# Two PSUM banks as one tile or as two: the weighted sums and the 3x3's products of an attention and convolution kernel

## The chip, the cores and the metric

The kernel runs on one core of a Trainium2 chip. The metric is the device time of one execution in microseconds (us). The runs before the change took 1933.58, 1933.69 and 1933.92 us; their median, 1933.69, is the time before.

## What is computed

The input x holds 8 images of 64 channels and 64 x 64 pixels in float32. Two layers follow each other:

```
# layer 0: attention over the 4096 pixels of each image
q, k, v = wq x + bq, wk x + bk, wv x + bv            # 64 x 64 weights
q, k    = q - mean(q), k - mean(k)                   # means over the pixels
out     = softmax(q^T k / 8) v                       # 4096 x 4096 scores
out    += (softmax(mean(q)^T k) v)                   # one row, added to every pixel
x       = x + out

# layer 1: binary convolutions with kernels of 1, 3 and 5
s = sum over k in (1, 3, 5) of bn_k(conv_k(sign(x + move_k), scale_k * sign(w_k - mean(w_k))))
gate = sigmoid(grouped linear map of mean(s) over the pixels)
x = s * gate + x
```

## The kernel before, in words

**Tiling.** Two images lie on the 128 partitions together, 64 channels each, so there are four pairs of images. A pair's 4096 queries are cut into eight blocks of 512 (`QB`), which makes 32 blocks, g = 0 to 31, in one long chain. Within a block the keys are taken 128 at a time in 32 steps (`NK`, index j).

**A step.** `scores` (lines 470 to 486) makes four matmuls of 64x64 weights and 512 columns into a PSUM tile of two banks; float32 matmuls appear twice in the records, so that a group of four in the code is a group of eight there. ScalarE takes the exponent of both banks in one instruction (line 485). `weighted` (lines 488 to 499) multiplies it with the values, in four matmuls of the same size, and adds the products over the 32 steps in the tile `acc`: two banks, one for each half h of the keys. VectorE adds up the exponents themselves (`summed`, line 508). Everything is written one step ahead: the scores of step j stand before the weighted sums of step j - 1, so the weighted sums of step 31 of a block come after the first scores of the next block.

**The hand-over between blocks.** `plan` (line 974) tells for each block what else stands at which step; the order of every engine's work is thus fixed by the program. At step 0 of block g these come, after the last weighted sums of block g - 1:

- `weighted_out` (lines 510 to 515): ScalarE copies the two banks of `acc` to SBUF, in one instruction of 128 x 1024 (line 515). The two halves are added together by VectorE some twelve steps later (`added`, line 582).
- `send` and `gather`: SyncE's DMAs for the sums of the exponents.
- `mix_rows` (lines 881 to 942): TensorE makes the queries of block g + 1 (line 460) and, from block 3 on, the convolution of block g - 3, as row products (line 703) of 256 columns in two interleaved sequences. One sequence has eight products S of the 5x5, the 1x1 (line 785), the twelve products of the 3x3 in the order A, B, S, D, three of each, and two more of the 5x5; the other has the 5x5's A, B and D. Each is made once for each image.
- The 3x3's A and B lie in the first bank of a tile, S and D in the second. This tile has the tag `acc`, of which the pool `ps_a` has one buffer: it is the same PSUM space as the weighted sums', which is empty between two blocks.
- When the 1x1 is done, `begin_rows` (line 729) has ScalarE scale it and put it in SBUF. When the last D product is recorded, `hold_rows` (lines 731 to 738) has ScalarE scale the whole 3x3 tile and put it in SBUF (line 734, 128 x 1024). VectorE adds the 5x5's products from PSUM (lines 744 and 750).

Then the scores of step 1 follow (line 474), and then the first weighted sums of block g (line 493), which write the tile with the tag `acc` again. Blocks 4, 12 and 20 have a small product ahead of these scores, for the means of the next pair (line 290), and blocks 8, 16 and 24 two, for the one-row softmax (line 363).

Dependencies are kept for each tile: an instruction that writes a tile anew waits for the last reader of the tile's former content, whichever of its banks that read.

**The end.** The last block is finished with the 2-D `mix` (line 830). Its attention result is copied out in two column parts (320 and 192 columns). For the first two blocks of output of the last pair, TensorE adds s * gate and x in a tile `pre` of two banks, also with the tag `acc` (lines 1103 to 1132): two products with the identity early on, two with the gate's diagonal at the very end, each followed by a copy by ScalarE (line 1131) and a store that ScalarE issues (line 1132). The other six blocks are done by VectorE (line 827) and stored by SyncE (line 828). A second path (lines 1171 to 1230) repeats the work with a safe softmax; it is skipped unless a sum went out of range.

Of the kernel before, what the change touches and what calls it, by code (L numbers as in the profile page):

```python
# [18 lines left out]
F32 = mybir.dt.float32  # L19
# [7 lines left out]
P = 128  # L27
C = 64
HH = 64
N = HH * HH  # L30
KS = (1, 3, 5)
QB = 512
# [12 lines left out]
def conv_seq_kernel(ctx, tc, x, wq, wk, wv, vecs, w1, w3, w5, wtap, gw, out):  # L45
    nc = tc.nc
# [3 lines left out]
    img = [slice(0, C), slice(C, P)]  # L50
# [6 lines left out]
    sm = ctx.enter_context(tc.tile_pool(name="small", bufs=2))  # L57
    dp = ctx.enter_context(tc.tile_pool(name="dram", bufs=2, space=bass.MemoryType.DRAM))
    ps_s = ctx.enter_context(tc.tile_pool(name="ps_s", bufs=2, space=PSUM))
    ps_a = ctx.enter_context(tc.tile_pool(name="ps_a", bufs=1, space=PSUM))  # L60
    ps_m = ctx.enter_context(tc.tile_pool(name="ps_m", bufs=2, space=PSUM))

    def m_tile(name):
        return ps_m.tile([P, QB], F32, tag="m", name=name)

    def load_x(name, rows, queues=(nc.sync,)):
        xt = xp.tile([P, N], F32, tag="x", name=f"x_{name}")
        for c in range(4):
            cols = bass.ts(c, N // 4)
            queues[c % len(queues)].dma_start(out=xt[:, cols], in_=xf[rows, cols])  # L70
        return xt
# [36 lines left out]
    ident = cp.tile([P, P], F32, tag="ident", name="ident")  # L108
# [42 lines left out]
    def warm(n):  # L151

        t = ps_s.tile([P, 2, QB], F32, tag="s", name="warm")[:, 0, :]
        for _ in range(n):
            nc.tensor.matmul(t[:, 0:P], ones, ones, start=True, stop=True)  # L155
# [89 lines left out]
    def n_products(k, name):  # L245
        return k if k == 3 or name == "D" else 2 * k
# [10 lines left out]
    class Pair:  # L257
# [229 lines left out]

        def weighted(self, qb, j, e):
            if j == 0:
                self.acc[qb] = ps_a.tile([P, 2, QB], F32, tag="acc", name=f"acc_{self.name}_{qb}")  # L490
            for b in range(2):
                for h in range(2):
                    nc.tensor.matmul(  # L493
                        self.acc[qb][img[b], h, :],
                        self.v[img[h], j, img[b]],
                        e[img[h], b, :],
                        start=(j == 0),
                        stop=(j == NK - 1),
                    )
# [10 lines left out]
        def weighted_out(self, qb, parts=(slice(0, QB),)):  # L510

            acc = self.acc[qb]
            self.acc[qb] = self.tile(fp, "o", qb, (P, 2, QB))
            for c in parts:
                nc.scalar.copy(self.acc[qb][:, :, c], acc[:, :, c])  # L515

# [209 lines left out]
            self.s[qb] = self.sum_tile(qb)  # L728
            nc.scalar.activation(self.s[qb], z, AF.Identity, bias=shift, scale=scale[:, 0:1])

        def hold_rows(self, qb, two):

            z = self.tile(sm, "es", f"z3_{qb}", (P, 2, QB))
            nc.scalar.activation(z, two, AF.Identity, scale=frac[3][:, 0:1])  # L734
            self.z3 = [
                z[:, i // 2, bass.ts(i % 2, QB // 2)].rearrange("p (j w) -> p j w", w=HH)
                for i in range(4)
            ]

        def add_rows(self, qb, a, b, s):  # L740
# [140 lines left out]
    def mix_rows(q, c):  # L881


        seqs = [[], []]
        if q is not None:
            for h in range(2):
                seqs[h].append((("q",), 0, 2.0))
        if c is not None:
            p, (r0, _, y) = c
            qb = r0 // ROWS  # L890

            def products(k, name):
                return [((k, name), i, 0.5) for i in range(n_products(k, name))]

            S = products(5, "S")
            three = [t for name in "ABSD" for t in products(3, name)]
            seqs[0] += S[:8] + [((1,), 0, 1.0)] + three + S[8:]
            seqs[1] += products(5, "A") + products(5, "B") + products(5, "D")
        order = []
        for h, seq in enumerate(seqs):  # L900
            at = 0.0
            for t in seq:
                order += [(at, h, b, t) for b in (h, 1 - h)]
                at += t[2]
        order.sort(key=lambda o: o[0:2])
        if q is not None:
            q[0].query_tiles(q[1])
        z, left = {}, {}
        for o in order:
            left[o[3][0]] = left.get(o[3][0], 0) + 1  # L910
        half = [slice(0, QB // 2), slice(QB // 2, QB)]
        for _, h, b, (n, i, _) in order:
            if n == ("q",):
                q[0].split_queries(q[1], b, h)
            else:
                if n not in z:
                    name = f"{p.name}_{qb}_{n[0]}"
                    if n == (1,):
                        z[n] = m_tile(f"z{name}")
                    elif n == (5, "D"):  # L920
                        z[n] = m_tile(f"z{name}d")[:, half[0]]
                    elif n[0] == 3:
                        z3 = ps_a.tile([P, 2, QB], F32, tag="acc", name=f"z{name}")
                        for j, m in enumerate("ABSD"):
                            z[3, m] = z3[:, j // 2, half[j % 2]]
                    else:
                        t = score_banks(f"z{name}")
                        z[5, "S"], z[5, "A"], z[5, "B"] = t[0][:, half[0]], t[1][:, half[0]], t[1][:, half[1]]
                if n == (1,):
                    p.conv_tap((r0, ROWS, y), [[z[n]]], b, 0, 0, 0, True, True)  # L930
                else:
                    p.row_product(z[n], b, *n, i, r0)
            left[n] -= 1
            if left[n] == 0 and n == ("q",):
                q[0].split_queries_out(q[1])
            elif left[n] == 0 and n == (1,):
                p.begin_rows(qb, z[n])
            elif left[n] == 0 and n == (3, "D"):
                p.hold_rows(qb, z3)
        if c is not None:  # L940
            p.add_rows(qb, z[5, "A"], z[5, "B"], z[5, "S"])
            p.z5d = z[5, "D"]
# [4 lines left out]
    def banks(pool, tag):  # L947
        def two(name):
            t = pool.tile([P, 2, QB], F32, tag=tag, name=name)
            return [t[:, 0, :], t[:, 1, :]]  # L950

        return two

    quarters = [slice(c * N // 4, (c + 1) * N // 4) for c in range(4)]
    acc_banks, score_banks = banks(ps_a, "acc"), banks(ps_s, "s")

    def misc_banks(name):
        return [m_tile(f"{name}_{h}") for h in range(2)]
# [5 lines left out]
    def attend(pairs):  # L964
# [9 lines left out]
        def plan(g):  # L974
# [17 lines left out]
            def both():  # L992
                q = block(g + 1) if g + 1 < n_blocks else None
                if g == 0:
                    mix(q, None)
                else:
                    mix_rows(q, rows(g - 3) if g >= 3 else None)
# [83 lines left out]
        for g in range(n_blocks):  # L1081
            pr, qb = divmod(g, NQ)
            at = plan(g)
            p = pairs[pr]
# [13 lines left out]
        p, b = pairs[-1], NQ - 1  # L1098
# [1 line left out]
        p.weighted_out(b, [slice(r0 * HH, r1 * HH) for r0, r1 in parts])  # L1100
        p.sums_wide(b)

        pre = ps_a.tile([P, 2, QB], F32, tag="acc", name="pre")
        for i in range(2):
            nc.tensor.matmul(pre[:, i, :], ident, p.x2[i], start=True, stop=False)
        warm(10)
        halves = [slice(r0 * HH, r1 * HH) for r0, r1 in parts]
        p.added(b, halves[0])
# [17 lines left out]
        diag_g = sm.tile([P, P], F32, tag="diag_g", bufs=1, name="diag_g")  # L1126
        nc.vector.tensor_scalar(diag_g, ident, p.gt, None, ALU.mult)
        rows_p = rows_of(n_pairs - 1)
        for i in range(2):
            nc.tensor.matmul(pre[:, i, :], diag_g, p.s[i], start=False, stop=True)  # L1130
            nc.scalar.copy(p.s[i], pre[:, i, :])
            nc.scalar.dma_start(out=of[rows_p, bass.ts(i, QB)], in_=p.s[i])
        for i in range(2, NQ):
            p.store(i, rows_p)
# [1 line left out]
    with tc.manual_schedule():  # L1136
        first = Pair("0", xt)
        warm(6)
        projection()
        warm(4)  # L1140
        first.mean_part(0, quarters[0])
        vectors()
        first.mean_part(1, quarters[1], True)
        first.mean_part(2, quarters[2])
        for c in range(2):
            first.mean_part(3 + c, slice(N * (6 + c) // 8, N * (7 + c) // 8), c == 1)
        first.query_tiles(0, score_banks)
        for b in range(2):
            first.queries(0, b)
        load_weights()  # L1150
        warm(18)
        first.mean_sum(5)
        first.mean_scores()
        first.mean_scores_out()
        first.queries_out(0)
        key_bias()
        first.value_weights()
        attend([first] + [None] * (n_pairs - 1))
# [12 lines left out]
    with tc.If(n_good < P):  # L1171
        neg = fp.tile([P, QB], F32, tag="e5", name="neg")
        nc.vector.memset(neg, 0.0)
        with tc.For_i(0, n_pairs * P, P) as row:
            rows = bass.ds(row, P)
            p = Pair("g", load_x("g", rows))
# [9 lines left out]
            for qb in range(NQ):  # L1186
                mix((p, qb), None)
                for h in range(QB // P):
                    part = sm.tile([P, 2, NQ], F32, tag="part", name=f"part_{qb}_{h}")
                    for kb_ in range(NQ):  # L1190
                        ps = ps_s.tile([P, 2, QB], F32, tag="s", name=f"px_{qb}_{h}_{kb_}")
                        for b in range(2):
# [4 lines left out]
                                start=True,  # L1197
                                stop=True,
# [90 lines left out]
```

## Time and profile before

The profile is of one execution on the chip. A busy share is the part of the span in which an engine had an instruction running; TensorE's matmuls overlap each other, and their ends are modelled.

| | before |
|---|---|
| median of 3 runs | 1933.69 us |
| the profiled execution's own time | 1934.02 us |
| its span, first to last instruction | 1931.8 us |
| TensorE busy | 1914.2 us, 20848 matmuls |
| VectorE busy | 1594.1 us |
| ScalarE busy | 1274.0 us, 1523 instructions |
| scores, line 474 | 8192 matmul records, 590 ns each |
| weighted sums, line 493 | 8192 matmul records, 590 ns each |
| exponents, line 485 | 1024 instructions, 1025 ns each |
| copies of the weighted sums, line 515 | 33 instructions, 31 of them 128 x 1024 at 1006 ns |
| copies of the 3x3's products, line 734 | 29 instructions, 1114 ns each |
| granted TensorE clock | 0.998 of full |

### The profile page before, as it was taken

How to read it: one execution, taken by the hardware profiler on the slowest of the kernel's cores; microseconds unless marked ns; L12 is line 12 of the kernel's file. 1: busy time of each engine (PE TensorE's matmuls, PEld its weight loads, DVE VectorE, ACT ScalarE, POOL GpSimd, SP SyncE). 2: the span in 40 equal slices, each digit the busy share in tenths (PEclk: the TensorE clock that was granted, in tenths of full speed). 3: DMA queues.
4: the chain of work that ended last, by engine and by line, in shares of the span. 5: the costliest groups of instructions: out<-in, count | busy, mean ns of one | idle time of the engine just before them, and what ended most of it. 6: DMA issues, size and time to landing. Idle time of an engine off the chain costs nothing.

```text
span 1931.8 us, 48355 instructions
## 1 busy us (share of the span) xinstructions
PE 1914.2 (99%) x20848; PEld 754.9 (39%) x20848; DVE 1594.1 (83%) x2066; ACT 1274.0 (66%) x1523; POOL 5.9 (0%) x26
## 2 busy tenths in 40 slices
PE   9999999999999999999999999999999999999997
PEld 4333343343333333343433333433443333333334
DVE  6878888889887888888888888898887888877876
ACT  5667766666666766666666676666666666666663
POOL 0000000000000000000000000000000000000000
PEclk9999999999999999999999999999999999999999
DMA  3021110110112110101101211011011011111111
GB/s 101 31 70 29 28 40 32 40 35 16 40 35 80 56 51 27 41 32 40 35 16 40 84 53 57 28 29 40 32 40 35 16 56 50 49 39 37 25 35 46
DMA packets 58998, 80.58 MB, mean 42 GB/s; under 512 B 15628, under 2 KB 40600, under 8 KB 58648
## 3 DMA queue, kind: packets, MB, share of 16 engines
q1 hardware_dynamic: 58024, 76.22, 12.9%
q8 instruction: 165, 2.70, 0.6%
q10 hardware_dynamic: 720, 1.18, 0.2%
q14 instruction: 57, 0.47, 0.1%
q0 software_dynamic: 32, 0.01, 0.0%
HBM read 39.27 MB, written 24.77 MB: 33 GB/s over the span
## 4 chain that ended last, share of the span: by engine, by line
PE 97%; DVE 1%; ACT 1%; DMA 0%; issue 0%; SPq 0%; DVEq 0%
PE ps L474 46%; PE acc L493 45%; PE z L703 4%; PE pv L313 1%; PE pq L460 1%; PE z L785 1%; ACT e L485 0%; DMA x<-in_x 0%; DVE es L508 0%; PE warm L155 0%; DVE r L576 0%; PE z_5d L703 0%; DMA out<-sb 0%; ACT o L515 0%; ACT rc_ck L418 0%
## 5 line engine op out<-in xcount | busy, mean ns | idle before, releaser
L485 ACT ACTIVATE e<-ps 128x1024 f32<-128x1024 f32 x1024 | 1049.7, 1025 | 597.8 <-PE ps L474 576.8
L508 DVE TENSOR_TENSOR es<-es,e 128x1024 f32<-128x1024 f32 x960 | 1171.2, 1220 | 187.6 <-ACT e L485 158.2
L474 PE MATMUL ps<-q,x 64*64 64x512 f32 x8192 | 1069.5, 590 | 0.9 <-DVE kb L165 0.9
L493 PE MATMUL acc<-e,v 64*64 64x512 f32 x8192 | 1065.2, 590 | 0.6 <-ACT e L485 0.3
L493 PEld LDWEIGHTS acc<-e,v 64*64 64x64 f32 x8192 | 307.6, 131 | 577.8 <-ACT e L485 305.9
L474 PEld LDWEIGHTS ps<-q,x 64*64 64x64 f32 x8192 | 312.2, 133 | 528.9 <-issue 278.0
L703 PE MATMUL z<-e,wt 64*64 64x256 bf16 x754 | 69.3, 270 | 0.1
L703 PE MATMUL z<-ec,wt 64*64 64x256 bf16 x754 | 69.4, 270 | 0.0
L744 DVE SCALAR_TENSOR_TENSOR sb<-z,scale,sb 128x256 f32<-128x256 f32 x29 | 14.0, 483 | 65.4 <-PE z L703 62.2
L703 PEld LDWEIGHTS <-wt 64*64 64x64 bf16 x1508 | 65.0, 105 | 0.4 <-issue 0.4
L703 PE MATMUL z<-ec,wc 64*64 64x256 bf16 x464 | 60.5, 270 | 0.0
L506 DVE TENSOR_TENSOR es<-e,e 128x1024 f32<-128x1024 f32 x32 | 39.2, 1225 | 24.5 <-ACT e L485 24.5
L703 PEld LDWEIGHTS <-wc 64*64 64x64 bf16 x1218 | 55.6, 106 | 4.8 <-issue 0.6
L619 ACT ACTIVATE s<-x,vec 128x512 bf16<-128x512 f32 (+2 forms) x66 | 46.1, 702 | 5.2 <-DVE x L587 5.2
L757 DVE TENSOR_TENSOR sb<-sb,es_z 128x256 f32<-128x256 f32 x116 | 43.9, 420 | 1.0
L703 PE MATMUL z<-e,wc 64*64 64x256 bf16 x319 | 44.4, 270 | 0.0
L734 ACT ACTIVATE es_z<-z,frac 128x1024 f32<-128x1024 f32 x29 | 32.3, 1114 | 16.3 <-PE z L703 16.3
L515 ACT COPY o<-acc 128x1024 f32<-128x1024 f32 (+2 forms) x33 | 32.3, 981 | 1.2 <-PE acc L493 1.2
L467 DVE TENSOR_SCALAR q<-pq,mx 128x256 f32<-128x256 f32 x30 | 14.5, 484 | 20.8 <-PE pq L460 20.8
L313 PEld LDWEIGHTS pv<-wx,x 64*64 64x64 f32 x1024 | 21.6, 134 | 17.8 <-issue 9.2
L703 PE MATMUL z<-s,wc 64*64 64x256 bf16 x145 | 25.4, 270 | 0.0
L587 DVE SCALAR_TENSOR_TENSOR x<-x,ou,x 128x512 f32<-128x512 f32 (+2 forms) x33 | 24.3, 735 | 1.2
(156 smaller groups left out, 743.6 us busy)
## 6 DMA issues: line engine op xcount, KB each, us to landing
es<-es SPq DMA_DIRECT2D x31, 512.0 KB
e_parts<-es SPq DMA_DIRECT2D x124, 128.0 KB
r<-rc SPq DMA_DIRECT2D x62, 128.0 KB
x<-in_x SPq DMA_DIRECT2D x15, 512.0 KB
out<-sb SPq DMA_DIRECT2D x28, 256.0 KB
ec<-e SPq DMA_DIRECT2D x29, 153.0 KB
xc<-in_x SPq DMA_DIRECT2D x60, 64.0 KB
ec<-e SPq DMA_DIRECT2D x29, 132.0 KB
```

Of the source, the lines that this page charges most:

```text
L313: nc.tensor.matmul(pv[img[h], b, i * w : (i + 1) * w], self.x[img[b], bass.ds((4 * g + i) * P + h * H, H)], self.wx[img[b], :], start=True ...
L474: nc.tensor.matmul(ps[img[h], b, :], self.x[img[b], bass.ds(j * P + h * H, H)], self.q[qb][img[b], :], start=True, stop=neg is None,)
L485: nc.scalar.activation(e, ps, AF.Exp, scale=1.0 / 8.0)
L493: nc.tensor.matmul(self.acc[qb][img[b], h, :], self.v[img[h], j, img[b]], e[img[h], b, :], start=(j == 0), stop=(j == NK - 1),)
L506: nc.vector.tensor_tensor(self.es[qb], self.first, e, ALU.add)
L508: nc.vector.tensor_tensor(self.es[qb], self.es[qb], e, ALU.add)
L515: nc.scalar.copy(self.acc[qb][:, :, c], acc[:, :, c])
L587: nc.vector.scalar_tensor_tensor(x2, x2, self.ou, self.x[:, bass.ts(qb, QB)][:, cols], ALU.add, ALU.add)
L619: nc.scalar.activation(sy[n][0][:, rows, pad : pad + HH], self.x2[qb][:, r0 * HH : r1 * HH].rearrange("p (h w) -> p h w", w=HH), AF.Sign, ...
L703: nc.tensor.matmul(z[img[b], :].rearrange("p (h w) -> p h w", w=HH), taps[img[h], c * C : c * C + C], src[:, first : first + 3 * step + 1 ...
L734: nc.scalar.activation(z, two, AF.Identity, scale=frac[3][:, 0:1])
L757: nc.vector.tensor_tensor(out, out, self.z3[i], ALU.subtract if (i, t) == (3, 1) else ALU.add)
```

## The change

The tile of two banks becomes two tiles of one bank each, with the tags `acc0` and `acc1`, wherever the tag `acc` was used: for the weighted sums, for the 3x3's products, and for `pre` at the end. The copy out of the weighted sums becomes two instructions of 512 columns, one for each bank. The 3x3's products are scaled and copied in two instructions too: the bank of A and B as soon as the last B product is recorded, the bank of S and D after the last D. Their place in SBUF stays one tile. The number and order of the matmuls stay.

```diff
         def weighted(self, qb, j, e):
             if j == 0:
-                self.acc[qb] = ps_a.tile([P, 2, QB], F32, tag="acc", name=f"acc_{self.name}_{qb}")
+                self.acc[qb] = acc_banks(f"acc_{self.name}_{qb}")
             for b in range(2):
                 for h in range(2):
                     nc.tensor.matmul(
-                        self.acc[qb][img[b], h, :],
+                        self.acc[qb][h][img[b], :],
...
             for c in parts:
-                nc.scalar.copy(self.acc[qb][:, :, c], acc[:, :, c])
+                for h in range(2):
+                    nc.scalar.copy(self.acc[qb][:, h, c], acc[h][:, c])
...
-        def hold_rows(self, qb, two):
-
-            z = self.tile(sm, "es", f"z3_{qb}", (P, 2, QB))
+        def hold_rows(self, qb, two, i):
+
+            if i == 0:
+                self.zh, self.z3 = self.tile(sm, "es", f"z3_{qb}", (P, 2, QB)), []
+            z = self.zh[:, i, :]
             nc.scalar.activation(z, two, AF.Identity, scale=frac[3][:, 0:1])
-            self.z3 = [
-                z[:, i // 2, bass.ts(i % 2, QB // 2)].rearrange("p (j w) -> p j w", w=HH)
-                for i in range(4)
+            self.z3 += [
+                z[:, bass.ts(t, QB // 2)].rearrange("p (j w) -> p j w", w=HH) for t in range(2)
             ]
...
-                        z3 = ps_a.tile([P, 2, QB], F32, tag="acc", name=f"z{name}")
+                        z3 = acc_banks(f"z{name}")
                         for j, m in enumerate("ABSD"):
-                            z[3, m] = z3[:, j // 2, half[j % 2]]
+                            z[3, m] = z3[j // 2][:, half[j % 2]]
...
-            elif left[n] == 0 and n == (3, "D"):
-                p.hold_rows(qb, z3)
+            elif left[n] == 0 and n in ((3, "B"), (3, "D")):
+                i = "BD".index(n[1])
+                p.hold_rows(qb, z3[i], i)
...
-    acc_banks, score_banks = banks(ps_a, "acc"), banks(ps_s, "s")
+    score_banks = banks(ps_s, "s")
+
+    def acc_banks(name):
+        return [ps_a.tile([P, QB], F32, tag=f"acc{h}", name=f"{name}_{h}") for h in range(2)]
...
-        pre = ps_a.tile([P, 2, QB], F32, tag="acc", name="pre")
+        pre = acc_banks("pre")
         for i in range(2):
-            nc.tensor.matmul(pre[:, i, :], ident, p.x2[i], start=True, stop=False)
+            nc.tensor.matmul(pre[i], ident, p.x2[i], start=True, stop=False)
...
-            nc.tensor.matmul(pre[:, i, :], diag_g, p.s[i], start=False, stop=True)
-            nc.scalar.copy(p.s[i], pre[:, i, :])
+            nc.tensor.matmul(pre[i], diag_g, p.s[i], start=False, stop=True)
+            nc.scalar.copy(p.s[i], pre[i])
```

## The prediction

> **What bounds the kernel now.** I read the page first, then the table of waits, then the timeline around the places where a block of 512 queries hands over to the next, then the same around the end. The page:
>
> ```profile
> PE 1914.2 (99%) x20848; PEld 754.9 (39%) x20848; DVE 1594.1 (83%) x2066; ACT 1274.0 (66%) x1523; POOL 5.9 (0%) x26
> ```
>
> TensorE is busy all the time, so what counts is time in which it could have started a matmul and did not. Busy time does not show that: each matmul record lasts longer than its distance from the next. The waits name the candidates (who waited for whom: us in total, times, longest):
>
> ```profile
> PEld acc L493 <- ACT e L485: 305.9, 955, 1.2
> ...
> PEld acc L493 <- ACT es_z L734: 22.2, 29, 0.9
> ```
>
> The second row is the wait that the change is about: the first weighted sum of a block waits for ScalarE to empty the 3x3's products (one allocation, both banks). But 22.2 us is idle time of the weight load, which is normally early; the first row has 305.9 us of it without harm. The timeline of one hand-over gives the true loss. Its columns are start, length, engine and line; first ScalarE's rows, then TensorE's:
>
> ```profile
> 779.64 1.01 ACT L515 COPY o<-acc 128x1024 f32<-128x1024 f32 x1
> 780.53 0.49 ACT L468 ACTIVATE q<-pq,nmx 128x256 f32<-128x256 f32 x1
> 781.07 0.78 ACT L729 ACTIVATE sb<-z,shift,scale 128x512 f32<-128x512 f32 x1
> 782.41 1.11 ACT L734 ACTIVATE es_z<-z,frac 128x1024 f32<-128x1024 f32 x1 [0.56 <-PE z L703]
> ```
>
> ```profile
> 782.55 1.03 PE L474 MATMUL ps<-q,x 64*64 64x512 f32 x6
> 783.58 1.09 PE L493 MATMUL acc<-e,v 64*64 64x512 f32 x8
> 784.49 1.04 PE L474 MATMUL ps<-q,x 64*64 64x512 f32 x8
> 785.34 1.04 PE L493 MATMUL acc<-e,v 64*64 64x512 f32 x8
> ```
>
> Undisturbed, groups of eight start 0.86 us apart (784.49 to 785.34), and a group starts 0.19 before the records of the one ahead end (784.49 + 1.04 = 785.53 against 785.34). The scores end at 782.55 + 1.03 = 783.58, so the weighted sums could start at 783.39. They start at 783.58, 0.06 after the copy ends at 783.52: 0.19 lost. The group after it follows 0.91 later, not 0.86: 0.05 more, seen whenever all eight loads go at once. Together **0.24 us per hand-over**.
>
> Where a small product stands between, nothing is lost: scores at 723.32, weighted sums 0.90 later, the next 0.86 after.
>
> ```profile
> 723.32 1.09 PE L474 MATMUL ps<-q,x 64*64 64x512 f32 x8
> 724.22 1.04 PE L493 MATMUL acc<-e,v 64*64 64x512 f32 x8
> 725.08 1.04 PE L474 MATMUL ps<-q,x 64*64 64x512 f32 x8
> ```
>
> Of the 29 blocks with 3x3 products (g = 3 to 31), six are like this (g = 4, 12, 20 with the means' scores, g = 8, 16, 24 with the unary sums). In the other 23 the timeline has the 0.91 after the weighted sums, each time.
>
> **What the Trainium skill says.** "Trainium Kernel Development and Optimization", Performance Expectations: matmul busy time is a bad measure, as matmuls are pipelined. The trace agrees: 99% busy with 0.24 us lost at 23 places. "ScalarE: Activation LUTs", What ACT_TABLE_LOAD costs: 186 ns + 0.833 ns a column, about 93 ns more for each pointer operand, and neighbours overlap by about 93 ns. The trace has 1114 ns for line 734 (1024 columns, one pointer; by the page 1132) and an overlap of 0.12 (copy at 779.64 for 1.01, next start 780.53). "PSUM — Partial Sum Buffer", PSUM bank collisions: two engines must not be in one bank and quadrant at once, different banks may be used together. That permits the split; no run here has shown it yet. "TensorE: Matmul & The Clock Gate", What's actually happening: after an idle window the clock is halved; the end of this trace agrees (part 4).
>
> **The change, part by part.** The order of instructions in the built program is the same on TensorE, VectorE and SyncE. ScalarE gets 62 more in the part that runs (33 copies of the sums, 29 of the products). TensorE gets one new ScalarE wait at the second weighted sum of a block and one at the first S product; the second of the last products (line 1130) loses its wait.
>
> 1. *The products' copy in halves.* The last D product starts at 782.09; A and B (bank 0) are complete six products of 0.11 earlier, at about 782.09 - 0.66 + 0.27 = 781.70. ScalarE is then in line 729 until 781.85 and idle until 782.41. So the first half starts at about 781.75, and nothing but the second half and the next exponent (783.64, set by the scores' end) is queued behind it. Half of line 734 is not in the trace: 0.59 (the plain 128x512 copy of line 321) to 0.78 (line 729, with two pointers). I take 1.114 - 512 x 0.833/1000 = 0.69. The first half ends at 782.44; the second starts when D is done, 782.41, and ends at 783.10. With 0.06 for the signal, bank 1 is free at 783.16, and at 783.25 with 0.78: both ahead of 783.39. The wait is gone, at either bound. Gain 0.24 in 22 blocks: 22 x 0.24 = 5.28 us.
>
> What is late next: the scores after these would start at 784.25 and need the score banks of the 5x5, whose last reader, VectorE's line 750, starts at 783.56 and takes 0.48, so 784.04, 0.10 for the signal at most: 0.11 to spare. Line 750 needs the second half too, now at 783.16. VectorE, 83% busy, catches up in each block (its sums wait 158.2 us for the exponents).
>
> 2. *The last block (g = 31)* has no queries ahead of the products, and there they wait for the sums' copy as well (ScalarE, then TensorE):
>
> ```profile
> 1839.71 1.01 ACT L515 COPY o<-acc 128x1024 f32<-128x1024 f32 x1
> ```
>
> ```profile
> 1840.42 0.61 PE L703 MATMUL z<-e,wt 64*64 64x256 bf16 x2
> 1840.77 0.29 PE L703 MATMUL z<-ec,wt 64*64 64x256 bf16 x1
> ```
>
> The pace of 0.11 breaks between 1840.42 and 1840.77, 0.05 after the copy ends. The products take 2.92 us to the next scores, 2.66 elsewhere. With bank 0 free at 1839.71 + 0.59 = 1840.30, A does not wait, and S (some 0.7 later) finds bank 1 free at 1840.79. Gain 0.26 + 0.24 = 0.50.
>
> 3. *The sums' copy in halves* elsewhere: 0.59 twice with 0.11 overlap, 1.07 for 1.01. The query half (line 468) starts 0.07 later. Its bank is next needed at 782.00, the queries a block later, and line 729 waits for the 1x1 (781.04). Nothing, covered by ScalarE's idle 0.69 a step; without that cover 31 x 0.07 = 2.2 us. At the very end, two copies of 320 columns (0.43 each) free the first addition at 1905.46 for 1905.39, and VectorE's chain stands on the path: -0.07.
>
> 4. *The last two products, in two tiles* (TensorE, SyncE's and ScalarE's stores, then the share of the 16 DMA engines in 40 slices of 1920 to 1931):
>
> ```profile
> 1920.48 1.12 PE L1130 MATMUL pre<-sb,diag_g 128*128 128x512 f32 x2 [0.83 <-DVE diag_g L1127]
> 1922.29 2.08 PE L1130 MATMUL pre<-sb,diag_g 128*128 128x512 f32 x2 [0.68 <-ACT sb L1131]
> ```
>
> ```profile
> 1923.77 1.25 SPq L828 DMA_DIRECT2D out<-es_j  x2
> ```
>
> ```profile
> 1925.01 0.35 ACTq L1132 DMA_DIRECT2D out<-sb  x1
> ```
>
> ```profile
> DMA  0000001798999999999999999963211300010100
> ```
>
> The second pair waits for the first copy and then takes 2.08 for 1.12, the halved clock that the skill tells of. Without the wait it starts at about 1921.4 and the last store is issued some 1.7 us sooner. But SyncE issues its own last until 1925.02, where ScalarE's ends at 1925.36, and the DMA engines are full from 1922 to 1927. So the gain is at most 0.34, at least nothing (no loss: the same bytes, none of them later). I take 0.2.
>
> Sum: 5.28 + 0.50 - 0.07 + 0.20 = **5.9 us**. The profiled execution took 1934.0 (span 1931.8 and 2.2 around it), 0.3 above the median of 1933.69: a span of 1925.9, a median of **1927.8** (-0.31%).
>
> **Rivals.** *Another wait takes over* (chance 0.15). VectorE's release of the 5x5's banks has only 0.11 to spare. If line 750 or its signal slips by 0.26, so 0.15 of the 0.24 is lost: 22 x 0.09 + 0.6 = 2.6 us, 1931.1. Against it: in this profile it already ends at 784.04 without help.
>
> *Nothing comes of it* (0.06). The 0.24 is given back inside each block, by VectorE not emptying the exponents' five buffers in time (that wait is 6.2 us in all now), or the two tiles still wait as one. Only the end's 0.1 remains: 1933.6. Against it: VectorE's slack, and the second weighted sum's own wait in the built program.
>
> *Slower* (0.06). ScalarE's fixed costs: if the first half is not released before D (the signal of B seen late), both halves run one after the other from 782.41: 0.58 + 0.69 = 1.27, ending 783.68 where the single one ended 783.52. That is 0.16 x 23 = 3.7 us, with the 0.07 of the end 1937.5. It decides from a first start later than 783.52 - 1.27 = 782.25. Against it: line 729 starts 0.03 after the 1x1's records end, so such signals are prompt.
>
> **How the numbers follow.** The forecast has 0.73: 0.67 within 1926.6 to 1930 (hand-over gain 0.17 to 0.29, the end 0 to 0.3), the rest at its lower edge. About 0.2% (3.9 us, so below 1929.8) is what a measurement of this kernel tells from no change. Faster by that: 0.72 of the forecast and 0.04 of the first rival, 0.76; within: 0.01, 0.11, 0.06 and 0.00, 0.18; slower: 0.06. The range goes to 1931.5 to take in the first rival.
>
> **What would show it.** Right: weighted sums 0.19 earlier after the scores and the 0.91 gone from behind them in 22 blocks; a first half at about 781.75 on the time base above; no row of weighted sums waiting for line 737 that costs a start; line 1130's second pair right behind the first. Wrong: first halves starting with D, or scores waiting for VectorE's line 753.

## The result and the profile after

The changed kernel takes 1928.79 us (median of 12 runs, 1927.98 to 1929.67), the kernel before 1933.66 us in the same series (median of 12, 1933.36 to 1934.51). The ratio is 0.9974, 95% interval 0.9966 to 0.9982: 0.26% faster, 4.9 us. The forecast was 1927.8.

The profiled execution took 1928.49 us, its span is 1926.3, 5.5 less than before. From its page, the busy times of the engines, then the two groups of copies (line, engine, operation, tiles, count; busy share or time, mean ns of one):

```profile
PE 1908.6 (99%) x20848; PEld 954.7 (50%) x20848; DVE 1592.5 (83%) x2066; ACT 1277.6 (66%) x1585; POOL 5.9 (0%) x26
...
L737 ACT ACTIVATE es_z<-z,frac 128x512 f32<-128x512 f32 x58 | 39.1, 687 | 0.0
L516 ACT COPY o<-acc 128x512 f32<-128x512 f32 (+2 forms) x66 | 34.4, 580 | 1.2 <-PE acc L493 1.2
```

The 62 more ScalarE instructions are there (1585 for 1523), and half of the products' copy takes 687 ns, where the forecast took 0.69. ScalarE is busy 3.6 us more, at no price. The table of waits of the changed kernel:

```profile
PEld acc L493 <- ACT e L485: 301.6, 955, 1.2
...
PEld acc L493 <- ACT es_z L737: 3.9, 22, 0.3
```

The second row was 22.2 us in 29 waits; what is left, 22 waits of 0.18 each, is a weight load that is early anyway. The hand-over that the prediction showed, now in the changed kernel, ScalarE and then TensorE (start, length, engine, line; `x2` is two instructions back to back):

```profile
778.39 1.07 ACT L516 COPY o<-acc 128x512 f32<-128x512 f32 x2
779.33 0.50 ACT L468 ACTIVATE q<-pq,nmx 128x256 f32<-128x256 f32 x1
779.82 0.78 ACT L730 ACTIVATE sb<-z,shift,scale 128x512 f32<-128x512 f32 x1
780.50 1.35 ACT L737 ACTIVATE es_z<-z,frac 128x512 f32<-128x512 f32 x2
```

```profile
781.17 0.60 PE L474 MATMUL ps<-q,x 64*64 64x512 f32 x2
...
781.30 1.03 PE L474 MATMUL ps<-q,x 64*64 64x512 f32 x6
782.03 1.15 PE L493 MATMUL acc<-e,v 64*64 64x512 f32 x8
782.89 1.15 PE L474 MATMUL ps<-q,x 64*64 64x512 f32 x8
783.75 1.15 PE L493 MATMUL acc<-e,v 64*64 64x512 f32 x8
```

The first half now starts behind line 730, 0.67 ahead of the scores, and both halves have ended at 781.85, before the weighted sums want their banks. These start 0.86 after the first two score records, the regular distance of two groups, and the next scores 0.86 after them: 1.72 in all. Before, the first two score records stood here:

```profile
782.43 0.60 PE L474 MATMUL ps<-q,x 64*64 64x512 f32 x2
```

The same three starts were then 782.43, 783.58 and 784.49, so 2.06. The hand-over itself is 0.34 us shorter, not 0.24.

The other 0.10 is only lent. The scores' records fall in two groups, 781.17 and 781.30, because one sequence of products ends 0.11 ahead of the other, so that one half of the array takes up the scores early. Before, the wait for the copy let the other half catch up: its groups behind the hand-over last 1.04. Now this lead is kept: the groups last 1.15 from then on. It is given back when products of another kind come between the groups: the mean's or the gate's (128*128, over the whole array), but also the values' (line 313, 64*64) and the 2-D convolution's in block 31. Why these end it isn't shown. The block with the mean's product (line 290) shows it, first before, then after:

```profile
720.11 0.27 PE L703 MATMUL z<-e,wc 64*64 64x256 bf16 x1
...
723.00 0.38 PE L290 MATMUL pm<-xm,mm 128*128 128x1 f32 x2
723.32 1.09 PE L474 MATMUL ps<-q,x 64*64 64x512 f32 x8
```

```profile
718.74 0.27 PE L704 MATMUL z<-e,wc 64*64 64x256 bf16 x1
...
721.75 0.38 PE L290 MATMUL pm<-xm,mm 128*128 128x1 f32 x2
722.06 1.09 PE L474 MATMUL ps<-q,x 64*64 64x512 f32 x8
```

From the first product to the mean's it is 2.89 before and 3.01 after: this block had no wait to lose, and pays 0.12. So the blocks, by the starts of their first scores, gain 0.34 where no such product comes (0.20 to 0.31 in blocks 28 to 30, where the lead from the block before is still there and grows to about 0.2), 0.24 where the values are made, 0.11 with the gate's product (blocks 10, 18 and 26), next to nothing with the one-row softmax's (8, 16 and 24), and lose 0.12 in the three with the mean's.

Block 31, ScalarE and then some of TensorE's products. The pace of 0.11 in one sequence runs on through the whole copy, which ends at 1836.03:

```profile
1834.96 1.07 ACT L516 COPY o<-acc 128x512 f32<-128x512 f32 x2
```

```profile
1835.91 0.29 PE L704 MATMUL z<-e,wt 64*64 64x256 bf16 x2
1835.97 0.31 PE L704 MATMUL z<-ec,wt 64*64 64x256 bf16 x2
1836.02 0.30 PE L704 MATMUL z<-e,wt 64*64 64x256 bf16 x2
1836.08 0.31 PE L704 MATMUL z<-ec,wt 64*64 64x256 bf16 x2
```

The hand-over of this block is 0.51 shorter, and the stretch behind it 0.18 longer, which is the lead again: the groups last 1.22 up to the 2-D convolution, 1.04 before the change. From the first scores of the program to the last sums over the exponents, the chain takes 1886.08 us after and 1891.71 before: **5.63 us less**, where parts 1 and 2 of the forecast have 5.78. By blocks it is 5.30 in blocks 3 to 30 and 0.51 less 0.18 in the last.

At the end (TensorE, ScalarE's store issues, then SyncE's), the four last products are one group without a wait:

```profile
1915.25 2.73 PE L1136 MATMUL pre<-sb,diag_g 128*128 128x512 f32 x4 [0.83 <-DVE diag_g L1133]
```

```profile
1917.03 0.36 ACTq L1138 DMA_DIRECT2D out<-sb  x1
...
1918.63 0.35 ACTq L1138 DMA_DIRECT2D out<-sb  x1
```

```profile
1915.88 2.32 SPq L830 DMA_DIRECT2D out<-sb  x4
1918.53 1.58 SPq L830 DMA_DIRECT2D out<-es_j  x2
```

ScalarE's last store is issued 2.75 after SyncE's first one; before, it was 3.89 (1925.01 against 1921.12). The span ends 10.46 after that first store, and before 10.67: 0.21 gained of 1.14. The span's 5.5 is then 5.63 + 0.21, less 0.39 by which the first scores came later in this execution (13.45 against 13.06, behind the landing of the first part of x). But the median fell by 4.9 only.

### The profile page after: what moved, and what is told of

Same layout as the page of the kernel before. It is cut to its first block, busy times and chain, and to the rows that moved or that the text cites. A ratio compares the mean times of both kernels' runs of the same rounds, so it can differ in the third digit from the quotient of the medians.

```text
span 1926.3 us, 48418 instructions
## 1 busy us (share of the span) xinstructions
PE 1908.6 (99%) x20848; PEld 954.7 (50%) x20848; DVE 1592.5 (83%) x2066; ACT 1277.6 (66%) x1585; POOL 5.9 (0%) x26
## 4 chain that ended last, share of the span: by engine, by line
PE 97%; DVE 1%; ACT 1%; DMA 0%; issue 0%; SPq 0%; DVEq 0%
PE ps L474 46%; PE acc L493 45%; PE z L704 4%; PE pv L313 1%; PE pq L460 1%; PE z L787 1%; DMA x<-in_x 0%; ACT e L485 0%; DVE es L508 0%; PE z_5d L704 0%; PE warm L155 0%; DVE r L577 0%; DVE sb L829 0%; ACT rc_ck L418 0%; DVE es_j L829 0%
## 5 line engine op out<-in xcount | busy, mean ns | idle before, releaser
L474 PE MATMUL ps<-q,x 64*64 64x512 f32 x8192 | 1136.7, 590 | 0.9 <-DVE kb L165 0.9
L493 PE MATMUL acc<-e,v 64*64 64x512 f32 x8192 | 1133.8, 589 | 0.6 <-ACT e L485 0.3
L474 PEld LDWEIGHTS ps<-q,x 64*64 64x64 f32 x8192 | 434.7, 133 | 407.4 <-issue 190.8
L493 PEld LDWEIGHTS acc<-e,v 64*64 64x64 f32 x8192 | 379.1, 131 | 501.3 <-ACT e L485 301.6
L737 ACT ACTIVATE es_z<-z,frac 128x512 f32<-128x512 f32 x58 | 39.1, 687 | 0.0
L516 ACT COPY o<-acc 128x512 f32<-128x512 f32 (+2 forms) x66 | 34.4, 580 | 1.2 <-PE acc L493 1.2
L467 DVE TENSOR_SCALAR q<-pq,mx 128x256 f32<-128x256 f32 x30 | 14.5, 484 | 19.7 <-PE pq L460 19.7
```

What stands on the lines that cost most here:

```text
L474: nc.tensor.matmul(ps[img[h], b, :], self.x[img[b], bass.ds(j * P + h * H, H)], self.q[qb][img[b], :], start=True, stop=neg is None,)
L493: nc.tensor.matmul(self.acc[qb][h][img[b], :], self.v[img[h], j, img[b]], e[img[h], b, :], start=(j == 0), stop=(j == NK - 1),)
L516: nc.scalar.copy(self.acc[qb][:, h, c], acc[h][:, c])
```

## Experiments

The theory: each hand-over's wait is gone because the bank of A and B is copied while D is still made, which needs two tiles as well as two copies. The rivals: the instruction order or the copies' speed does it rather than the overlap; or the sums' copy carries part of the gain; or the 0.73 between the six scores and the weighted sums is a gain of another kind. All times are medians, with the ratio to the kernel before and its 95% interval.

### The changed kernel again

> The changed kernel once more, for a second trace and as the ground for its neighbours in this call. If the gain is the hand-overs' wait, the weighted sums start 0.7 to 0.75 us after the six-record group of the scores in the blocks from 3 on, as in the first trace (1.02 before), and the median is 1928.8 +- 0.5. If the 0.65 us by which the median gain (4.9) stays behind that of the two profiled executions (5.5) is in the hand-overs, this trace has blocks with a longer group; if it is in the start or the end, the hand-overs are alike and the start of the first scores or the stretch after the last weighted sums differs.

1928.81 us (1928.47 to 1929.38, 10 runs), 0.9974 (0.9965 to 0.9984). Its chain is 1886.10. The gain and the chain repeat; its end does not, and is taken up below.

### Both halves written behind the last D

```diff
-            elif left[n] == 0 and n in ((3, "B"), (3, "D")):
-                i = "BD".index(n[1])
-                p.hold_rows(qb, z3[i], i)
+            elif left[n] == 0 and n == (3, "D"):
+                for i in range(2):
+                    p.hold_rows(qb, z3[i], i)
```

> Both halves of the products are copied after the last D product, one behind the other; all else as in the changed kernel. Theory (the early first half is what takes the wait away): the second half ends 1.27 us after D in place of 0.69, the second weighted sum waits for it, about 0.39 us more at each of 23 hand-overs, 8.6 us: 1937.4, slower than the kernel before. Rival (what counts is that each bank waits only for its own copy, whenever it is made): the first weighted sum starts on bank 0 and the rest follows, 1929 to 1931.

1928.58 us (1927.99 to 1931.23, 8 runs), 0.9975 (0.9965 to 0.9986): nothing lost, and my expectation of 1937.4 was wrong. ScalarE's timeline at the same hand-over says why:

```profile
779.36 0.78 ACT L730 ACTIVATE sb<-z,shift,scale 128x512 f32<-128x512 f32 x1
780.04 1.35 ACT L737 ACTIVATE es_z<-z,frac 128x512 f32<-128x512 f32 x2
```

The first half still starts right behind line 730. No other ScalarE instruction stands between the two places, and the one that moved waits for the last writer of its own tile, B, wherever it is written. ScalarE's order of work is the same as in the changed kernel, so this tests nothing of the overlap: it is in effect a third trace of the changed kernel.

### The bank of S and D first, both after D

Here the overlap is really taken away: the first of the two copies needs D, and the other is queued behind it. (`hold_rows` is turned round to match; that part of the edit is left out here.)

```diff
...
-            elif left[n] == 0 and n in ((3, "B"), (3, "D")):
-                i = "BD".index(n[1])
-                p.hold_rows(qb, z3[i], i)
+            elif left[n] == 0 and n == (3, "D"):
+                for i in (1, 0):
+                    p.hold_rows(qb, z3[i], i)
```

> The changed kernel, with the bank of S and D copied first (after D, as it must) and the bank of A and B behind it, so that both copies really come after D. In the run before this, the early half kept its place although it was issued later in the program, since it waits for B alone; so that run did not try it. Theory (the early half takes the wait away): bank 0, which the first weighted sum needs, is free 1.27 + 0.06 us after D, 0.16 later than with the one copy before: +3.7 us in 23 hand-overs on the kernel before, less 0.3 in the last block: 1937. Rival (smaller tiles are enough): 1929.

1937.47 us (1936.62 to 1939.49, 14 runs), 1.0020 (1.0012 to 1.0028): slower than before. ScalarE, then TensorE:

```profile
783.28 1.26 ACT L737 ACTIVATE es_z<-z,frac 128x512 f32<-128x512 f32 x2 [0.56 <-PE z L704]
```

```profile
783.30 0.60 PE L474 MATMUL ps<-q,x 64*64 64x512 f32 x2
783.42 1.03 PE L474 MATMUL ps<-q,x 64*64 64x512 f32 x6
784.60 1.09 PE L493 MATMUL acc<-e,v 64*64 64x512 f32 x8
785.51 1.04 PE L474 MATMUL ps<-q,x 64*64 64x512 f32 x8
```

The halves run after the products, 1.26 for both, and the weighted sums start 0.06 after they end. The three starts are 1.30 and 0.91 apart, 2.21 in all, 0.15 more than before, in each of the 22 hand-overs; the blocks with the mean's product or the one-row softmax's lose nothing. The edit also changes which bank is copied last, but that can't be what counts: the first four records of the weighted sums, which write both banks, start within 0.02 us (784.60 to 784.62). The chain is 3.16 longer than before. Same instructions, same tiles: the difference to the changed kernel, 1937.47 - 1928.79 = 8.7 us, is the overlap, 22 x (0.24 + 0.15) = 8.6 by the hand-overs in the traces.

### Two copies, but one tile

```diff
-        def hold_rows(self, qb, two):
+        def hold_rows(self, qb, two, i):
...
-            elif left[n] == 0 and n == (3, "D"):
-                p.hold_rows(qb, z3)
+            elif left[n] == 0 and n in ((3, "B"), (3, "D")):
+                i = "BD".index(n[1])
+                p.hold_rows(qb, z3[:, i, :], i)
```

(an edit of the kernel before; the sums' copy stays whole)

> The kernel before, with the products copied in the two halves (after B and after D) but left in one tile of two banks; sums and last products as before. Theory (the tiles are what lets TensorE go on): the first S product now waits for the first half's copy, as the program shows a wait there; it starts at the copy's end and 0.06, 0.96 us late. The later wait of the weighted sums is gone (-0.24 in 23 blocks). 23 x 0.72 + 6 x 0.96 = 22 us: 1956. Rival (two copies alone do it): 1928 to 1929.

1956.15 us (1955.89 to 1956.43, 4 runs), 1.0116 (1.0100 to 1.0131), 22 us slower than before. Its table of waits has a new row, and the timeline shows it between two products (ScalarE's half from 789.86 to 790.55):

```profile
PE z L703 <- ACT es_z L736: 21.6, 29, 0.8
```

```profile
789.86 0.69 ACT L736 ACTIVATE es_z<-z,frac 128x512 f32<-128x512 f32 x1
```

```profile
789.57 0.27 PE L703 MATMUL z<-e,wt 64*64 64x256 bf16 x1
790.60 0.27 PE L703 MATMUL z<-e,wc 64*64 64x256 bf16 x1 [0.77 <-ACT es_z L736]
```

S writes the tile that the copy of A and B reads, in another bank, and waits for it. Two copies without two tiles cost 22 us; with two tiles they gain 4.9.

### The sums' second bank first

```diff
-                for h in range(2):
+                for h in (1, 0):
                     nc.scalar.copy(self.acc[qb][:, h, c], acc[h][:, c])
```

> The copies of the weighted sums change places, so that bank 0, which the 3x3's A product needs first, comes free as late as in the kernel before. Theory: this matters in the last block alone, where the products come without queries ahead of them, 0.26 to 0.3 us: 1929.1. Rival (a good part of the gain is that the products start on bank 0 sooner): 0.1 us or more at each of 29 hand-overs, 1931.7 or more.

1929.13 us (1928.12 to 1930.29, 12 runs), 0.9975 (0.9966 to 0.9983). Only block 31 differs in the trace: A's bank comes free last, and TensorE's pace breaks there. ScalarE's copies, then the products:

```profile
1835.32 1.07 ACT L516 COPY o<-acc 128x512 f32<-128x512 f32 x2
```

```profile
1836.03 0.27 PE L704 MATMUL z<-ec,wt 64*64 64x256 bf16 x1
1836.04 0.66 PE L704 MATMUL z<-e,wt 64*64 64x256 bf16 x2
1836.44 0.29 PE L704 MATMUL z<-ec,wt 64*64 64x256 bf16 x1
```

Here 1836.44 is 0.05 after the second copy ends. The block gains 0.10 instead of 0.51. In the other blocks it is the same which half of the sums comes first, as part 3 of the forecast has it. The 0.3 us in the median is what the trace says, but within the noise.

### The two sequences of products made equally long

To test the lead of one half of the array: the shorter sequence gets one more product on each image, a tap of S that is made twice, so that both end together.

```diff
-            seqs[0] += S[:8] + [((1,), 0, 1.0)] + three + S[8:]
+            seqs[0] += S[:8] + [((1,), 0, 1.0)] + three + S[8:9] + S[8:]
```

> The changed kernel with one S product of the 5x5 made twice in each row convolution (the output holds that tap twice), so that the two sequences of the hand-over are of one length: 58 products more. Seen in the traces: the half of the array with the shorter sequence starts the scores 0.11 us ahead of the other and stays ahead, and the weighted sums come 0.73 after the scores' group in place of 0.84, until a product that needs the whole array gives the 0.10 back (+0.12 in the blocks with the means' product). Theory (the longer sequence sets the pace, the lead is worth nothing): 0 to 0.5 us, 1928.8 to 1929.3, and no 0.73 any more. Rival (every product costs its 0.11): 29 x 0.11 = 3.2 us, 1932.0.

1929.79 us (1928.73 to 1931.96, 21 runs), 0.9980 (0.9974 to 0.9987). TensorE's hand-over:

```profile
783.85 1.04 PE L474 MATMUL ps<-q,x 64*64 64x512 f32 x8
784.71 1.04 PE L493 MATMUL acc<-e,v 64*64 64x512 f32 x8
785.57 1.08 PE L474 MATMUL ps<-q,x 64*64 64x512 f32 x8
```

The scores are one group of eight, the 0.86 is regular, and no 0.73 is left: the lead is made by the unequal sequences. The median is 1.0 above the changed kernel's, more than the 0 to 0.5 expected. The chain is 0.83 longer (1886.91), about 0.03 a block, far from the 3.2 of the rival: most of the 58 products fill room that the longer sequence had left beside them. So the lead is worth 0.83 at the very most, and how much of that is the added products' own time isn't separated.

### TensorE's branch later

In the changed kernel TensorE hands out the last four products without a wait and begins the branch ahead of the skipped second path 2.0 us earlier than before (16.3 us after the last sums over the exponents instead of 18.4). Behind it the records of the instruction queue (`q8 instruction`) show a transfer of 16 KB. One more product of 128 columns, waiting for the second copy, holds the branch back to 19.7; a second kernel also has eight more of the dummy products ahead of the last ones, to keep TensorE's clock up.

```diff
             nc.scalar.dma_start(out=of[rows_p, bass.ts(i, QB)], in_=p.s[i])
+        nc.tensor.matmul(pre[0][:, 0:P], ident, p.s[1][:, 0:P], start=True, stop=True)
```

> The changed kernel with one product of 128 columns more behind the last two, which reads what ScalarE's second copy wrote. TensorE's branch behind them, and the fetch of instructions that it sets off, then come as late as before the change. The stretch from the sums of the last exponents to the end was 27.0 and 27.2 us in the two traces with the old end and 26.8, 27.3, 27.7, 27.8 in the four with the new one, in which the fetch falls among SyncE's stores and the third of these takes up to 2 us to issue. Theory A (the early fetch costs the 0.4): the third store issues in 0.4, the stretch is 26.6 to 26.9, the median 1928.3. Theory B (it is where TensorE's clock is halved, before the last products in three of these four): the fetch moves but the stretch stays, 27.4; 1928.8.

```diff
         mix(None, (p, p.joint_rows(11, 16)), one_bank, score_banks)
+        warm(8)
         p.check(p.r[b], n_blocks - 1)
```

> As late_branch, and TensorE is kept busy with 8 idle products of 128 columns behind the last convolution, so that its clock is less likely to be halved before the last two products. Theory A: no shorter than late_branch, 26.6 to 26.9. Theory B: the pair of last products takes 1.1 us and not 2.1 to 2.2, and the stretch 26.5 to 26.9 here alone: 1928.2, where late_branch has 1928.8.

1928.33 us (1927.84 to 1929.88, 10 runs), 0.9974 (0.9964 to 0.9983), and 1928.19 us (1927.55 to 1930.38, 9 runs), 0.9973 (0.9963 to 0.9983). SyncE's first four stores in three kernels, the changed one again, the one with equal sequences, and the late branch:

```profile
1915.82 3.36 SPq L830 DMA_DIRECT2D out<-sb  x4
```

```profile
1919.03 3.61 SPq L830 DMA_DIRECT2D out<-sb  x4
```

```profile
1915.61 2.32 SPq L830 DMA_DIRECT2D out<-sb  x4
```

All profiles side by side, in us. The transfer, ScalarE's last store and the end are counted from the start of SyncE's first store; the two middle columns are lengths:

| kernel | instruction transfer behind the branch starts | SyncE's first four issues take | the last four products take | ScalarE's last store is issued | span ends |
|---|---|---|---|---|---|
| before | 3.8 | 2.32 | 1.12 and 2.08 | 3.9 | 10.67 |
| two copies, one tile | 4.1 | 2.32 | 1.12 and 2.07 | 3.9 | 10.80 |
| after | 2.1 | 2.32 | 2.73 | 2.8 | 10.46 |
| after, again | 1.1 | 3.36 | 3.78 | 3.8 | 10.80 |
| both halves behind D | 1.0 | 3.91 | 3.66 | 3.7 | 11.35 |
| sums' second bank first | 1.0 | 4.01 | 3.78 | 3.8 | 11.20 |
| S and D's bank first | 1.0 | 4.11 | 3.78 | 3.8 | 11.50 |
| equal sequences | 1.0 | 3.61 | 1.98 | 2.2 | 10.78 |
| late branch | 5.8 | 2.32 | 1.98 | 2.2 | 10.17 |
| late branch, warm | 5.7 | 2.32 | 1.98 | 2.2 | 10.31 |

In the five where the transfer starts 1.0 or 1.1 after the first store, the third issue takes 1.5 to 2.0 us instead of 0.33. In the five where it comes later, none does. Six profiles have the changed kernel's end (rows 3 to 8): 11.01 on average, where the two with the old end have 10.67 and 10.80. That is 0.28 later, where the forecast had 0.2 sooner. In all six TensorE's branch begins 0.04 before SyncE's first store; why the transfer follows 1.1 later in five of them and 2.1 later in the first profile is open.

With the branch held back the end is at 10.24 on average. Theory A's numbers came nearly so: the third issue takes 0.33, the stretch from the last sums over the exponents to the end is 26.5 and 26.7, and the medians are 1928.33 and 1928.19 against 1928.79 and 1928.81. But the intervals overlap, so the time alone doesn't show it.

The clock is part of the spread too. The Trainium skill, "TensorE: Matmul & The Clock Gate", What's actually happening, tells that TensorE falls to half its clock after an idle window. In the changed kernel's second profile that had come before the last products:

```profile
1915.19 3.78 PE L1136 MATMUL pre<-sb,diag_g 128*128 128x512 f32 x4 [0.83 <-DVE diag_g L1133]
```

The same four take 1.98 with the branch late, and 2.73 in the first profile. In four of the six profiles they take 3.66 to 3.78, and ScalarE's last store is then issued only 0.1 or 0.2 us sooner than before. Both profiles with the late branch have 1.98, with and without the eight dummy products, so the second kernel shows nothing more, and part of the 10.24 is the clock's. The kernel with equal sequences also has 1.98, and still a slow third issue: the clock does not make the issue slow. With these products alike, the two kernels with the late branch end 0.6 and 0.5 sooner than that one, by one profile each.

## Why the prediction held, and where not

**Part 1, right in sum, the hand-over's form a little off.** The forecast was 22 x 0.24 = 5.28; with part 2 the chain gives 5.63 of 5.78. The half copy (687 ns), the first half's start behind line 730 and the vanished 0.91 are as forecast. Off was the place that the weighted sums would reach: 0.84 after the six scores, measured 0.73. The forecast counted from the later of the two groups of scores, and the weighted sums follow the earlier one at 0.86. That gave 0.34 in place of 0.24, and the 0.10 went back later, as shown above. The Trainium skill's "PSUM — Partial Sum Buffer", PSUM bank collisions, lets two engines use different banks at once. The trace now shows it: TensorE starts the products S and D on one image at 780.51, 780.62, 780.73 and 780.84, at the undisturbed pace of 0.11, while ScalarE reads the bank of A and B from 780.50. The first two of them:

```profile
780.51 0.27 PE L704 MATMUL z<-e,wc 64*64 64x256 bf16 x1
780.62 0.27 PE L704 MATMUL z<-e,wc 64*64 64x256 bf16 x1
```

**What was to be late next** was VectorE's release of the 5x5's banks, with 0.11 to spare. VectorE's row:

```profile
782.25 0.48 DVE L752 SCALAR_TENSOR_TENSOR es_z<-z,frac,es_z 128x256 f32<-128x256 f32 x1
```

It ends at 782.73, 0.16 ahead of the scores at 782.89, though these start earlier than forecast, and no row of scores waiting for it is in the table of waits. The first rival did not come.

**Part 2, right:** 0.50 forecast, 0.51 measured in the block; 0.18 of lead, carried in from the blocks before (their groups last 1.22 too), is given back behind it. In the kernel with equal sequences, which has hardly any lead, the block is 0.45 shorter. The sums' second bank first takes away the larger part, 0.41, as the two waits of the forecast say.

**Part 3, right for the blocks:** turning the two halves around changes none but block 31. The 0.07 at the very end was wrong, but small: VectorE's first addition does start 0.05 later (0.67 after the last sums over the exponents instead of 0.62), but the reciprocals that follow start 1.13 after them in both profiles, and SyncE's first store 16.35. The addition doesn't set VectorE's pace there.

**Part 4, wrong.** The step that failed is "no loss: the same bytes, none of them later". Without the wait TensorE also begins its branch sooner, and in five of six profiles the instruction transfer that follows falls among SyncE's store issues, one of which then takes 1.5 to 2.0 us. The other step, that ScalarE's last store comes "some 1.7 us sooner", took it for granted that the last products run at the full clock: it was so in one profile of the six, and in four it came 0.1 or 0.2 sooner. Instead of 0 to 0.34 gained, the six profiles end between 0.2 sooner and 0.8 later than the one before the change, and on average 0.28 later than the two with the old end. With the first profile's end alone one would have called part 4 right (0.21 gained).

**The sum:** 5.63 from the chain less 0.28 at the end is 5.35, and 4.9 was measured, with 3.5 to 6.6 in its interval. The rest is not settled: the start of the first scores varies from 12.9 to 13.8 us among nine of the profiles, is 15.75 in the one with equal sequences, and was seen in one execution of each kernel (two of the changed one) only.

**The rival on the other side was priced well.** Both halves after D: 1.27 forecast for the two copies, 1.26 measured, 0.16 per hand-over forecast and 0.15 measured, 1937.5 forecast and 1937.47 measured. That the totals agree so closely is luck: the chain is 3.16 longer where the forecast had 3.7, and the end, at 11.50 for 10.67 in its profile, made up for it. It needed another order of the copies to happen, since a copy's start is set by the last writer of its own bank.

## What to carry to other kernels

Two PSUM banks that are filled one after the other were worth two tiles and two copies here, because the engine that copies was idle while the second filled: the price is 0.06 to 0.15 us for the second instruction (1.07 for 1.01, 1.26 for 1.11), the gain is the overlap; splitting the copy without the tile cost 22 us. When a wait at the very end is removed, look at what the freed engine does next, a branch and its instruction transfer included, and take more than one profile of the end before believing a few tenths.

## What the runs showed of the hardware

- Halves of TensorE's array that get unequal sequences of 64x64 products run apart by their difference (0.11 us here), keep that lead through some 60 groups of records (lengths of 1.15 for 1.04), and give it back when other products come between: a 128x128 product (3.01 for 2.89), but also the values' 64x64 products (lengths of 1.04 again).
- A transfer of instructions of 16 KB (0.9 to 1.9 us) that starts about 1 us after SyncE's first store goes with an issue of 1.5 to 2.0 us in place of 0.33. With the transfer moved to 5.7 or 5.8 after the store the issue takes 0.33 again (two profiles); by which path the one delays the other is open.
